# A gated graph layer on one core: five pieces of vector work change engines and tiles are aggregated two at a time

## The chip, the cores and the metric

The kernel runs on one core of a Trainium2 chip. The metric is the device time of one execution in microseconds (us), as the median of three runs. A core has a matrix engine (TensorE, PE in the profile, with PEld for its weight loads), a vector engine (VectorE, DVE), an engine for activations and copies (ScalarE, ACT), a general engine (GpSimd, POOL) and one that only issues transfers (SyncE, SP). Each engine works through its own queue in order, and the engines wait for each other through semaphores.

## What is computed

For each of 16 graphs there are 1024 nodes with 256 features (x), and one sparse 1024 x 1024 matrix A (adj) is shared by all. The weights W1 have two halves of 256 rows. For every edge from u to v with A[u, v] not zero, a gate is computed from both ends, and the node v sums the features of its neighbours once with A alone (m) and once with A times the gate (a):

```python
pre_u = jnp.einsum('bud,dk->buk', h_t, W1[:d])
pre_v = jnp.einsum('bvd,dk->bvk', h_t, W1[d:])
hidden = jax.nn.relu(pre_u[:, :, None, :] + pre_v[:, None, :, :] + b1)
S = jax.nn.sigmoid(jnp.einsum('buvk,ko->buvo', hidden, W2)[..., 0] + b2[0])
a_t = jnp.einsum('buv,bud->bvd', S * A_a, h_t)
m_t = jnp.einsum('uv,bud->bvd', A_m, h_t) * h_t
z_t = beta1 * h_t + beta2 * (jnp.einsum('bvd,de->bve', a_t, Wa) + ba) + beta3 * (jnp.einsum('bvd,de->bve', m_t, Wm) + bm)
```

The kernel visits only the edges that exist, about nine per node.

## The kernel before

**Blocks and tiles.** The 16 graphs are four groups (g) of four (GB), and the 1024 nodes are eight tiles of 128 (vt). A block k is one pair (g, vt), so there are 32 blocks. A block has two windows w of 64 nodes, and a window's edges fill five tiles of 128 edge slots (TW = 5). So a block has ten tiles, and the main loop (L684) runs over n = 0 to 319, one tile a step, with s = n % 10 as the place in the block. The order in which each engine gets its instructions is the order in which this loop writes them; `after(step, f)` puts a piece of work off to a later step, where `do(n)` writes it.

**A tile's way.** For tile n:

- `fetch` (L451): GpSimd issues an indirect transfer that gathers 128 rows of 8 KB from a table in DRAM into one of five SBUF buffers `fetched` (NF = 5). Half of a row is h W1[:D] of node u for four graphs, the other half is h of node u.
- `expand` (L518): two PE products of the 0/1 matrix `mark` with X give, for each slot, h W1[D:] + b1 of its node v, in a PSUM tile `pc` of two banks. There are two such tiles (psc, bufs=2).
- `gate` (L536): DVE adds the fetched half and `pc` into an SBUF tile `t` (L539), then takes, graph by graph, the positive part times the row W2 and its sum (L543, four instructions, each followed by one that reads the accumulator). ACT makes the sigmoid (L546) and four scaled copies (L549).
- `left_adj` (L527): ACT writes the other half of the weights `left`: the 0/1 columns `onehot` times the edge's value `val` (L533).
- `aggregate` (L551): PE multiplies `left` (32 columns per graph) with the fetched h, four or eight products a tile, into sums `acc` in PSUM. The profile counts each of these products twice, so a tile shows as x8 or x16.

In step n the loop writes: aggregate(n-1), then fetch(n+4) into the buffer that this has freed, then gate(n), left_adj(n+1), whatever was put off to this step, and expand(n+2). After these come the pieces of the block work:

- `halves(k+1)` (L409): X of the next block. PE computes h W1[D:] + b1 in two halves; ACT copies each to X, rounded for the PE (L418), and DVE takes the rest, that is the PSUM value minus X (L419, `low`). ACT copies both to their places in X (L422, L425). These are written at s = 0, 2, 3, 4, 6.
- `half_end`, `turn_over` (L565, L570): ACT copies finished sums from PSUM (L568), PE transposes them (L578), ACT copies the result to `LT` (L581), and DVE multiplies the m part with h transposed (L591, `times_h`).
- `block_end(k-1)` (L596), at s = 3 to 6: PE multiplies `LT` with Wm and Wa on top of a bias row (L608, `pz`); DVE forms z = beta1 h + pz in place in the SBUF tile `h_blk` (L612), and SyncE writes that to DRAM.
- `rows` (L391): for the tables of later groups, PE computes h W1[:D]; the last piece is written in step 231.
- `lists` (L236) finds the edges of a node tile, mainly on DVE. Four of the eight run before the main loop, the others within its first hundred steps. GpSimd also fetches the edge values (`fetch_val`, L338), two per step, as long as some are left.

So GpSimd had the transfers alone, and DVE had per block ten gates, two L419, two L591 and two L612.

Of the kernel before, what the change touches and what calls it, by code (L numbers as in the profile page):

```python
# [13 lines left out]
P = 128  # L14
# [3 lines left out]
def kernel(  # L18
# [390 lines left out]
    def halves(k):  # L409
        X = cuts[k] = big.tile([P, NW, GD], FR, name="X")  # L410
        low = one.tile([P, GD], FR, name="low")
        for h in range(2):
# [6 lines left out]
            after(step + 1, lambda c=c, p=p: nc.vector.tensor_tensor(  # L419
                low[:, c], p, X[:, 0, c].bitcast(FP), ALU.subtract))  # L420
        yield
        nc.scalar.copy(X[W:, 1, :], X[W:, 0, :].bitcast(FP))  # L422
        for w in range(NW):
            yield
            nc.scalar.copy(X[(1 - w) * W:(2 - w) * W, w, :], low[w * W:(w + 1) * W].bitcast(FP))  # L425
# [85 lines left out]

    marks, pcs, accs, evs, hbs, LTs, lefts = {}, {}, {}, {}, {}, {}, {}
# [14 lines left out]
    def left_adj(n):  # L527
# [4 lines left out]
        lefts[n] = wk.tile([P, 2, GB, 2, V], FP, name="left")  # L532
        nc.scalar.activation(lefts[n][:, :m, :, 0, :], onehot[:, i, o:o + m, :].unsqueeze(2).to_broadcast([P, m, GB, V]),  # L533
                             AF.Copy, scale=val[:, i, j:j + 1])

    def gate(n):  # L536
        k, g, vt, w, j = where(n)
        t = one.tile([P, GB, D], FP, name="t")
        nc.vector.tensor_tensor(t, fetched[n % NF][:, :GD].rearrange("p (b d) -> p b d", b=GB),  # L539
                                pcs.pop(n).rearrange("p (b d) -> p b d", b=GB), ALU.add)  # L540
# [6 lines left out]
        for b in range(GB):  # L547
            m = len(QUARTERS[j])
            nc.scalar.activation(lefts[n][:, :m, b, 1, :], lefts[n][:, :m, b, 0, :], AF.Copy, scale=gt[:, b:b + 1])  # L549

    def aggregate(n):  # L551
        k, g, vt, w, j = where(n)
        left, f = lefts.pop(n), fetched[n % NF]
        for i, q in enumerate(QUARTERS[j]):
# [4 lines left out]
            for b in range(GB):  # L559
                nc.tensor.matmul(accs[h][b * 2 * V:(b + 1) * 2 * V, r, :],  # L560
                                 left[:, i, b].rearrange("p k v -> p (k v)"), f[:, GD + b * D:GD + (b + 1) * D],
                                 start=first, stop=(j == q + 1), skip_group_check=True)
# [7 lines left out]
    def turn_over(k, w, q, step):  # L570
# [18 lines left out]
        def times_h():  # L589
            m = LT[:, :, :, 0, v]  # L590
            nc.vector.tensor_tensor(m, m, hTs[order[k]].rearrange("p b c n -> p c b n")[:, :, :, v], ALU.mult)  # L591
# [4 lines left out]
    def block_end(k):  # L596

        g, vt = order[k]
        hb = hbs[k]
        for h in range(2):  # L600
            for bb in range(2):
# [4 lines left out]
                for i, wt in enumerate((w_m, w_a)):  # L606
                    for c in range(DC):
                        nc.tensor.matmul(pz[:, bb * D:(bb + 1) * D], LTs[k][:, c, 2 * h + bb, i, :], wt[:, c, :],  # L608
                                         start=False, stop=(i == 1 and c == DC - 1), skip_group_check=True)

            def add(h=h, pz=pz):
                nc.vector.scalar_tensor_tensor(hb[:, 2 * h:2 * h + 2, :], hb[:, 2 * h:2 * h + 2, :], be1,  # L612
                                               pz.rearrange("p (b d) -> p b d", b=2), ALU.mult, ALU.add)
# [263 lines left out]
```

## Time and profile before

The median is 1183.41 us (1183.29 to 1184.95). The profiled execution has a span of 1195.2 us[...]. The main loop starts at 68.5 us (the first L539) and the last gate starts at 1174.2 us.

| group | times | mean, ns |
|---|---|---|
| L419 DVE, rest of h W1[D:] | 64 | 686 |
| L591 DVE, m times h (128x512) | 55 | 688 |
| L612 DVE, z | 62 | 744 |
| L533 ACT, left | 320 | 364 |
| L546 ACT, sigmoid | 320 | 298 |
| L549 ACT, four per tile | 1280 | 304 |
| L568, L581 ACT, copies from PSUM of 128x512 | 128 each | 587, 575 |
| L418 ACT, copy from PSUM to X, 128x512 | 64 | 583 |
| L453 POOL, issue of a gather | 320 | 1030 |
| L341 POOL, issue of an edge value fetch | 80 | 1046 |

In such a profile an engine's busy time is the union of its instructions' spans. Two instructions that follow each other overlap at their ends, so the distance from one start to the next says more about what an instruction costs its engine than its duration does. "Idle before" is the time that an engine stood still just ahead of a group, with the instruction whose end released it. A wait in the table costs time only if the waiting engine is the one that sets the pace at that place.

### The profile page before, as it was taken

Reading aid. Unit: us, or ns where it says so; the run is one execution under the profiler, and the core shown is the slowest. Engines: PE = TensorE matmul, PEld = TensorE weight load, DVE = VectorE, ACT = ScalarE, POOL = GpSimd, SP = SyncE. Lnnn points to the kernel's source line nnn. Section 1 sums busy time; section 2 is a strip of 40 time slices with the busy share of each in tenths; the row PEclk is TensorE's granted clock in tenths of the full one; section 3 lists DMA queues with packets and bytes.
Section 4 is the critical chain, followed back from the end, with each engine's and each line's share of the span. In section 5 each row is a group of like instructions: output and inputs, shape, how many; then the busy total and the mean of one; then the engine's idle time right before and its main releaser. Section 6 shows DMA issues by size and latency. Waiting matters only on the chain. (4 is left out here: it accounts for less than half of the span.)

```text
span 1195.2 us, 23788 instructions
## 1 busy us (share of the span) xinstructions
PE 1097.9 (92%) x7633; PEld 724.7 (61%) x7633; DVE 1066.9 (89%) x3515; ACT 840.4 (70%) x2498; POOL 426.1 (36%) x428
## 2 busy tenths in 40 slices
PE   7667988999889898999999999999999999999986
PEld 6544655666556565666666666666666666666653
DVE  8769879989988988899899999999999999999994
ACT  3346666677667665777777777787878777777873
POOL 1557652433263226333233333333333333333330
PEclk9968899999999999999999999999999999999998
DMA  9988889899979978999999999999999999999992
GB/s 279 312 307 261 258 319 333 315 336 377 320 254 373 361 244 302 357 384 360 351 329 379 359 331 371 362 356 386 358 367 345 356 324 326 326 341 328 335 340 76
DMA packets 147046, 391.39 MB, mean 327 GB/s; under 512 B 16752, under 2 KB 105328, under 8 KB 110704
## 3 DMA queue, kind: packets, MB, share of 16 engines
q0 software_dynamic: 50016, 300.50, 68.5%
q1 hardware_dynamic: 81616, 74.99, 19.6%
q10 hardware_dynamic: 15280, 14.29, 3.7%
q8 instruction: 63, 1.03, 0.3%
q14 instruction: 71, 0.58, 0.1%
HBM read 393.78 MB, written 50.33 MB: 372 GB/s over the span
## 5 line engine op out<-in xcount | busy, mean ns | idle before, releaser
L453 POOL DMA_INDIRECT fetched<-table,uidx x320 | 329.7, 1030 | 675.5 <-PE acc L560 509.6
L543 DVE SCALAR_TENSOR_TENSOR t<-t,w_b 128x256 f32<-128x256 f32 x1280 | 469.3, 422 | 20.1 <-ACT LT L581 0.5
L539 DVE TENSOR_TENSOR t<-fetched,pc 128x1024 f32<-128x1024 f32 x320 | 388.8, 1215 | 22.4 <-DMA fetched<-table,uidx 8.6
L560 PE MATMUL acc<-fetched,left 128*32 128x256 f32 x4096 | 334.2, 394 | 32.3 <-ACT left L549 16.8
L549 ACT ACTIVATE left<-left,gt 128x32 f32<-128x32 f32 (+1 forms) x1280 | 299.4, 304 | 10.4
L523 PE MATMUL pc<-X,mark 128*128 128x512 f32 x640 | 238.1, 454 | 21.1 <-DVE t L539 13.6
L560 PEld LDWEIGHTS acc<-fetched,left 128*32 128x32 f32 x4096 | 129.9, 110 | 177.2 <-issue 46.9
L546 ACT ACTIVATE gt<-sc,b_b 128x4 f32<-128x4 f32 x320 | 95.3, 298 | 140.5 <-DVE t L543 133.9
L523 PEld LDWEIGHTS pc<-X,mark 128*128 128x128 f32 x640 | 97.2, 191 | 156.6 <-issue 102.2
L608 PE MATMUL misc<-w_a,LT 128*128 128x256 f32 x496 | 127.3, 379 | 0.0
L608 PE MATMUL misc<-w_m,LT 128*128 128x256 f32 x496 | 127.1, 378 | 0.0
L384 PE MATMUL misc<-w_u,hT 128*128 128x256 f32 x448 | 109.2, 390 | 11.0 <-ACT few L298 3.6
L533 ACT ACTIVATE left<-onehot,val 128x128 f32<-128x128 bf16 (+1 forms) x320 | 116.5, 364 | 0.0
L384 PE MATMUL misc<-w_v,hT 128*128 128x256 f32 x448 | 107.9, 384 | 0.0
L543 DVE DVE_READ_ACCUMULATOR t<-t,w_b 128x1 f32 x1280 | 104.2, 81 | 0.0
L608 PEld LDWEIGHTS misc<-w_m,LT 128*128 128x128 f32 x496 | 93.7, 189 | 17.2
L384 PEld LDWEIGHTS misc<-w_u,hT 128*128 128x128 f32 x448 | 85.8, 195 | 27.3 <-issue 4.4
L608 PEld LDWEIGHTS misc<-w_a,LT 128*128 128x128 f32 x496 | 94.2, 190 | 12.8
L568 ACT COPY ev<-acc 128x512 f32<-128x512 f32 x128 | 75.1, 587 | 34.7 <-PE acc L560 26.8
L341 POOL DMA_INDIRECT val<-in_adjT_dram,vidx x80 | 83.6, 1046 | 33.4 <-issue 21.9
L384 PEld LDWEIGHTS misc<-w_v,hT 128*128 128x128 f32 x448 | 86.7, 194 | 14.3
L581 ACT COPY LT<-misc 128x512 f32<-128x512 f32 x128 | 71.1, 575 | 24.0 <-PE pc L523 12.0
(158 smaller groups left out, 830.9 us busy)
## 6 DMA issues: line engine op xcount, KB each, us to landing
h_blk<-in_x_dram SPq DMA_DIRECT2D x31, 512.0 KB
out_dram<-h_blk SPq DMA_DIRECT2D x31, 512.0 KB
hT<-in_xT_dram SPq DMA_DIRECT2D x28, 512.0 KB
table<-tab SPq DMA_DIRECT2D x26, 512.0 KB
table<-in_x_dram ACTq DMA_DIRECT2D x24, 512.0 KB
fetched<-table,uidx POOLq DMA_INDIRECT x320
table<-in_x_dram SPq DMA_DIRECT2D x8, 512.0 KB
table<-fetched SPq DMA_DIRECT2D x6, 512.0 KB
```

The costliest lines, as they stand in the source:

```text
L341: nc.gpsimd.indirect_dma_start(out=val[:, i, j:j + 1], out_offset=None, in_=adj_flat, in_offset=bass.IndirectOffsetOnAxis(ap=vidx[:, i, j: ...
L384: nc.tensor.matmul(p[:, bb * D:(bb + 1) * D], hT[:, 2 * h + bb, i, :], wt[:, i, :], start=(i == 0 and not begun), stop=(i == DC - 1), skip ...
L453: nc.gpsimd.indirect_dma_start(out=fetched[n % NF], out_offset=None, in_=table[g], in_offset=bass.IndirectOffsetOnAxis(ap=uidx[:, vt * NW ...
L523: nc.tensor.matmul(pcs[n][:, c], marks[n // TW][:, j * P:(j + 1) * P], cuts[k][:, w, c], start=True, stop=True)
L533: nc.scalar.activation(lefts[n][:, :m, :, 0, :], onehot[:, i, o:o + m, :].unsqueeze(2).to_broadcast([P, m, GB, V]), AF.Copy, scale=val[:, ...
L539: nc.vector.tensor_tensor(t, fetched[n % NF][:, :GD].rearrange("p (b d) -> p b d", b=GB), pcs.pop(n).rearrange("p (b d) -> p b d", b=GB), ...
L543: nc.vector.scalar_tensor_tensor(t[:, b, :], t[:, b, :], 0.0, w2_b, ALU.max, ALU.mult, accum_out=sc[:, b:b + 1])
L546: nc.scalar.activation(gt, sc, AF.Sigmoid, bias=b2_b)
L549: nc.scalar.activation(lefts[n][:, :m, b, 1, :], lefts[n][:, :m, b, 0, :], AF.Copy, scale=gt[:, b:b + 1])
L560: nc.tensor.matmul(accs[h][b * 2 * V:(b + 1) * 2 * V, r, :], left[:, i, b].rearrange("p k v -> p (k v)"), f[:, GD + b * D:GD + (b + 1) * D ...
L568: nc.scalar.copy(evs[q], accs.pop(q))
L608: nc.tensor.matmul(pz[:, bb * D:(bb + 1) * D], LTs[k][:, c, 2 * h + bb, i, :], wt[:, c, :], start=False, stop=(i == 1 and c == DC - 1), sk ...
```

## The change

Six edits are made together. (1) `left` times `val` goes from ACT to GpSimd, with four buffers in place of three. (2) The rest of h W1[D:]: ACT now copies the PSUM value to SBUF a second time (`low`), and GpSimd subtracts X from it; the first block keeps DVE. (3) `times_h` goes from DVE to GpSimd, but for the last block. (4) z: ACT copies pz to a new SBUF tile `z`, GpSimd scales h and adds; the products with Wa come ahead of those with Wm, so that the m part is needed later. (5) The sum of fetched half and `pc` is written over `pc` in PSUM, and the gate works there, in place. (6) Tiles are aggregated two at a time: in every even step n the loop writes aggregate(n-2) and aggregate(n-1), and the two fetches n+3 and n+4; in odd steps it writes neither. A piece of `halves` moves from s = 4 to s = 5.

The purpose is to take everything from DVE but the gates, to let GpSimd do elementwise work between its transfers, and to let PE change less often between kinds of products. GpSimd is given SBUF operands only, and the copies in (2) and (4) provide them.

```diff
@@ -408,7 +408,8 @@
 
     def halves(k):
         X = cuts[k] = big.tile([P, NW, GD], FR, name="X")
-        low = one.tile([P, GD], FR, name="low")
+        low = one.tile([P, GD], FP, name="low")
+        engine = nc.gpsimd if k else nc.vector
         for h in range(2):
             step = yield
             c = slice(2 * h * D, (2 * h + 2) * D)
@@ -416,13 +417,13 @@
             add_row(p, b1_p)
             half_product(p, hTs[order[k]], w_v, h, True)
             nc.scalar.copy(X[:, 0, c], p)
-            after(step + 1, lambda c=c, p=p: nc.vector.tensor_tensor(
-                low[:, c], p, X[:, 0, c].bitcast(FP), ALU.subtract))
+            nc.scalar.copy(low[:, c], p)
+            after(step + 1, lambda c=c: engine.tensor_tensor(low[:, c], low[:, c], X[:, 0, c].bitcast(FP), ALU.subtract))
         yield
         nc.scalar.copy(X[W:, 1, :], X[W:, 0, :].bitcast(FP))
         for w in range(NW):
             yield
-            nc.scalar.copy(X[(1 - w) * W:(2 - w) * W, w, :], low[w * W:(w + 1) * W].bitcast(FP))
+            nc.scalar.copy(X[(1 - w) * W:(2 - w) * W, w, :], low[w * W:(w + 1) * W])
 
     engines = mybir.EngineType
     main.enter_context(tc.manual_schedule(
@@ -529,15 +531,16 @@
         i = vt * NW + w
         m = len(QUARTERS[j])
         o = max(2 * j - 1, 0)
-        lefts[n] = wk.tile([P, 2, GB, 2, V], FP, name="left")
-        nc.scalar.activation(lefts[n][:, :m, :, 0, :], onehot[:, i, o:o + m, :].unsqueeze(2).to_broadcast([P, m, GB, V]),
-                             AF.Copy, scale=val[:, i, j:j + 1])
+        lefts[n] = wk.tile([P, 2, GB, 2, V], FP, name="left", bufs=4)
+        nc.gpsimd.tensor_scalar(lefts[n][:, :m, :, 0, :], onehot[:, i, o:o + m, :].unsqueeze(2).to_broadcast([P, m, GB, V]),
+                                val[:, i, j:j + 1], None, ALU.mult)
+
 
     def gate(n):
         k, g, vt, w, j = where(n)
-        t = one.tile([P, GB, D], FP, name="t")
-        nc.vector.tensor_tensor(t, fetched[n % NF][:, :GD].rearrange("p (b d) -> p b d", b=GB),
-                                pcs.pop(n).rearrange("p (b d) -> p b d", b=GB), ALU.add)
+        m = len(QUARTERS[j])
+        t = pcs.pop(n).rearrange("p (b d) -> p b d", b=GB)
+        nc.vector.tensor_tensor(t, fetched[n % NF][:, :GD].rearrange("p (b d) -> p b d", b=GB), t, ALU.add)
         sc = wk.tile([P, GB], FP, name="sc")
         for b in range(GB):
             nc.vector.scalar_tensor_tensor(t[:, b, :], t[:, b, :], 0.0, w2_b,
@@ -545,7 +548,6 @@
         gt = wk.tile([P, GB], FP, name="gt")
         nc.scalar.activation(gt, sc, AF.Sigmoid, bias=b2_b)
         for b in range(GB):
-            m = len(QUARTERS[j])
             nc.scalar.activation(lefts[n][:, :m, b, 1, :], lefts[n][:, :m, b, 0, :], AF.Copy, scale=gt[:, b:b + 1])
 
     def aggregate(n):
@@ -557,8 +559,8 @@
             if first:
                 accs[h] = psa.tile([P, 2, D], FP, name=f"acc{h}")
             for b in range(GB):
-                nc.tensor.matmul(accs[h][b * 2 * V:(b + 1) * 2 * V, r, :],
-                                 left[:, i, b].rearrange("p k v -> p (k v)"), f[:, GD + b * D:GD + (b + 1) * D],
+                nc.tensor.matmul(accs[h][b * 2 * V:(b + 1) * 2 * V, r, :], left[:, i, b].rearrange("p k v -> p (k v)"),
+                                 f[:, GD + b * D:GD + (b + 1) * D],
                                  start=first, stop=(j == q + 1), skip_group_check=True)
@@ -588,7 +590,7 @@
 
         def times_h():
             m = LT[:, :, :, 0, v]
-            nc.vector.tensor_tensor(m, m, hTs[order[k]].rearrange("p b c n -> p c b n")[:, :, :, v], ALU.mult)
+            (nc.vector if k == BS - 1 else nc.gpsimd).tensor_tensor(m, m, hTs[order[k]].rearrange("p b c n -> p c b n")[:, :, :, v], ALU.mult)
             if w == NW - 1 and q == 1:
                 del hTs[order[k]]
         after(step + 1, times_h)
@@ -597,23 +599,27 @@
 
         g, vt = order[k]
         hb = hbs[k]
+        z = big.tile([P, GB, D], FP, name="z", bufs=1)
         for h in range(2):
             for bb in range(2):
                 step = yield
                 if bb == 0:
                     pz = small("pz")
                     add_row(pz, bias_p)
-                for i, wt in enumerate((w_m, w_a)):
+                for i, wt in ((1, w_a), (0, w_m)):
                     for c in range(DC):
                         nc.tensor.matmul(pz[:, bb * D:(bb + 1) * D], LTs[k][:, c, 2 * h + bb, i, :], wt[:, c, :],
-                                         start=False, stop=(i == 1 and c == DC - 1), skip_group_check=True)
-
-            def add(h=h, pz=pz):
-                nc.vector.scalar_tensor_tensor(hb[:, 2 * h:2 * h + 2, :], hb[:, 2 * h:2 * h + 2, :], be1,
-                                               pz.rearrange("p (b d) -> p b d", b=2), ALU.mult, ALU.add)
+                                         start=False, stop=(i == 0 and c == DC - 1), skip_group_check=True)
+
+            sl = slice(2 * h, 2 * h + 2)
+            nc.scalar.copy(z[:, sl], pz.rearrange("p (b d) -> p b d", b=2))
+
+            def add(sl=sl):
+                nc.gpsimd.tensor_scalar(hb[:, sl], hb[:, sl], be1, None, ALU.mult)
+                nc.gpsimd.tensor_tensor(z[:, sl], hb[:, sl], z[:, sl], ALU.add)
             after(step + 1, add)
         after(step + 2, lambda: nc.sync.dma_start(
-            out[g * GB:(g + 1) * GB, vt * P:(vt + 1) * P, :].rearrange("b p d -> p b d"), hb))
+            out[g * GB:(g + 1) * GB, vt * P:(vt + 1) * P, :].rearrange("b p d -> p b d"), z))
         del hbs[k], LTs[k]
@@ -684,12 +690,15 @@
     for n in range(total + 2):
         k, s = divmod(n, T)
         if 1 <= n <= total:
-            aggregate(n - 1)
             fetch_val(2)
-            if n - 1 + NF < total:
-                fetch(n - 1 + NF)
-            if n % TW in (0, MID + 1):
-                half_end(n - 1, 0 if n % TW else 1)
+        if 2 <= n <= total and n % 2 == 0:
+            for i in (n - 2, n - 1):
+                aggregate(i)
+                if i + NF < total:
+                    fetch(i + NF)
+            for i in (n - 2, n - 1):
+                if i % TW in (MID, TW - 1):
+                    half_end(i, 0 if i % TW == MID else 1)
         if n < total:
             gate(n)
             if n + 1 < total:
@@ -741,7 +750,7 @@
             next(end)
             go(end, n)
             go(end, n)
-        if k + 1 < BS and s in (0, 2, 3, 4, 6):
+        if k + 1 < BS and s in (0, 2, 3, 5, 6):
             if s == 0:
                 parts = halves(k + 1)
                 next(parts)
```

## The prediction

> **What bounds the kernel now.** I read the page's busy line first, then its costliest groups, then the busy time by stage, then timelines of one block.
>
> The page, busy time and groups:
>
> ```profile
> PE 1097.9 (92%) x7633; PEld 724.7 (61%) x7633; DVE 1066.9 (89%) x3515; ACT 840.4 (70%) x2498; POOL 426.1 (36%) x428
> ...
> L453 POOL DMA_INDIRECT fetched<-table,uidx x320 | 329.7, 1030 | 675.5 <-PE acc L560 509.6
> L543 DVE SCALAR_TENSOR_TENSOR t<-t,w_b 128x256 f32<-128x256 f32 x1280 | 469.3, 422 | 20.1 <-ACT LT L581 0.5
> L539 DVE TENSOR_TENSOR t<-fetched,pc 128x1024 f32<-128x1024 f32 x320 | 388.8, 1215 | 22.4 <-DMA fetched<-table,uidx 8.6
> L560 PE MATMUL acc<-fetched,left 128*32 128x256 f32 x4096 | 334.2, 394 | 32.3 <-ACT left L549 16.8
> ```
>
> PE and DVE are both near full and hardly idle; POOL is idle two thirds of the time, waiting for PE to free a gather buffer. Which of the two sets the pace depends on the stage. Busy time by stretch (columns: length, then busy time and instructions of PE, PEld, DVE, ACT, POOL; granted clock; DMA share; GB/s):
>
> ```profile
> 68.50:532.70 464.20, 419.59 (x2841) 277.58 (x2841) 410.51 (x1365) 315.13 (x937) 198.70 (x195) 0.95 0.90 316
> 532.70:927.70 395.00, 386.92 (x2765) 253.67 (x2766) 363.46 (x1152) 306.13 (x922) 124.08 (x121) 1.00 0.98 358
> 927.70:1176.60 248.90, 237.07 (x1714) 149.58 (x1716) 239.62 (x765) 191.72 (x594) 78.53 (x77) 1.00 0.92 326
> ```
>
> The cuts are starts of blocks: 12 early blocks of 38.7 us (edge lists on DVE), 12 middle ones of 32.9 us (tables for later groups on PE) and 8 late ones of 31.1 us. Late, DVE is busy 96%; in the middle PE is busy 98%. The timelines of DVE and PE in a late block:
>
> ```profile
> 1083.31 1.22 DVE L539 TENSOR_TENSOR t<-fetched,pc 128x1024 f32<-128x1024 f32 x1
> 1084.56 0.42 DVE L543 SCALAR_TENSOR_TENSOR t<-t,w_b 128x256 f32<-128x256 f32 x1
> 1084.91 0.08 DVE L543 DVE_READ_ACCUMULATOR t<-t,w_b 128x1 f32 x1
> ...
> 1088.84 0.69 DVE L419 TENSOR_TENSOR low<-misc,X 128x512 fp32r<-128x512 f32 x1
> 1089.44 1.21 DVE L539 TENSOR_TENSOR t<-fetched,pc 128x1024 f32<-128x1024 f32 x1
> ...
> 1105.23 1.03 PE L608 MATMUL misc<-w_m,LT 128*128 128x256 f32 x4
> 1106.09 1.03 PE L608 MATMUL misc<-w_a,LT 128*128 128x256 f32 x4
> 1107.05 1.07 PE L560 MATMUL acc<-fetched,left 128*32 128x256 f32 x16
> 1108.05 0.73 PE L523 MATMUL pc<-X,mark 128*128 128x512 f32 x2
> 1108.62 1.03 PE L578 MATMUL misc<-ident,ev 128*128 128x128 f32 x8
> 1109.59 1.07 PE L560 MATMUL acc<-fetched,left 128*32 128x256 f32 x16
> ```
>
> From start to start, a gate costs DVE 1.25 for the sum and 4 x 0.35 = 1.40, so 2.65 us. L419 costs 0.60, and so (timeline) do L591 0.61 and L612 0.66. A block's DVE work is 26.5 + 2 x (0.60 + 0.61 + 0.66) = 30.2 of 31.1 us. On PE an aggregation costs 1.00 (x16) or 0.57 (x8), an expansion 0.57, two L608 groups 1.82, eight transposes 0.97. Per block: 6 x 1.00 + 4 x 0.57 + 10 x 0.57 + w_v 2 x 1.82 + four bias rows 0.92 + L608 4 x 1.82 + transposes 2.1 = 27.9 us; with two pieces of `rows`, 31.5. So DVE bounds the late blocks (30.2 of 31.1) and PE the middle ones (31.5 of 32.9), each with about 1 us of coupling.
>
> A third loop runs through the gathers. By the semaphores in the trace, a gather lands 6.3 us (late) to 6.9 us (middle) after its issue ends, on average; 5.5 us when the one before it had 1 to 2 us left to run. It lands only 2.5 to 1.9 us before its gate starts.
>
> [...]
>
> **The change part by part.**
>
> Off DVE: 2 x 1.87 = 3.7 us per block, for 31 blocks nearly. Left: 26.5 us.
>
> In place in PSUM: before shows DVE reading PSUM (L539 1215 ns, against 1219 ns for L244 of the same size from SBUF), so a read costs nothing; a write to PSUM is nowhere. Lower bound 0[...]. I take 0.1 us per tile, as reads show none of it: DVE 27.5 per block[...]. The edit also holds `pc` until the gate's end: expand(n+2), which waited for L539, now waits 1.4 us longer, and queued behind it on PE are that step's block pieces and expand(n+3). The gate of tile n+1 runs meanwhile on the other `pc`, and gate n+2 is due 2.65 us later, while an expansion takes 0.57. I cost it at nothing on DVE.
>
> ACT: off, 10 x 0.364 = 3.6 us; on, 4 copies of 128x512 at 0.58 (L418) = 2.3. 1.3 less of 24 (191.7/8); ACT stays below 26 us, also in the middle (306.1/12 = 25.5).
>
> POOL, per block: ten gathers 10.3 (L453); ten `left`; two subtractions, two m x h, two scalings and two sums of 512 columns. Bounds: DVE's 0.69 us for the same sum (L591) below[...]. I take 1.15 for the six two-input ones (6.9), 0.6 for the scalings (1.2), and 0.3 for a `left` of 64 or 128 elements (3.0; between the 0.16 us memset L205 and ACT's 0.36). Sum 21.4 us of 31 (18 to 25): not a bound. POOL's order matters more: in even steps two issues (2.1 us), then left(n+1), then the odd work. In the first 15 steps two value fetches per step (2.1 us) come on top: 1.0 + 2.1 + 1.1 = 4.2 us of the 4.4 us that those steps take.
>
> New waits. The Wm products of L608 wait for m x h on POOL, which ends 2.1 + 0.3 + 1.15 = 3.6 us after the pair's aggregation; PE reaches them after two expansions, a `halves` piece, a bias row and the Wa products, 0.57 + 2.05 + 0.57 + 0.23 + 0.87 = 4.3 us after it, so nothing; behind them is the next pair. ACT's L549 of tile n+1 waits for its `left`, 2.4 us after the aggregation, while that gate ends later than 4 us after it; behind L549 on ACT are copies and the next sigmoid: nothing. POOL's sums of z wait for ACT's copy of pz, and the next two issues stand behind them: up to 0.5 us at s = 6 and 8, in the range.
>
> PE: 16 records take 1.00 and 8 take 0.57, so a change of kind costs 0.14; five pairs save 0.7 per block. PE: 27.2 late, 30.8 middle.
>
> Pairing the gathers. Before: issue 1.0, landing 6.3, gate 2.65, sigmoid and scaling 1.3 (0.30 + the four L549 0.96), aggregation 1.0: 12.3 us over five tiles, 24.5 per block. After: the first gather of a pair is issued a step later, so the same chain must close over four tiles. With a nearly empty transfer queue (5.5): 11.5 us per four tiles, 28.8 per block; with 6.3 us, 30.6. This eats most of what DVE gives free.
>
> Sum. Late: bounds DVE 27.5, PE 27.2, gathers 28.8; plus the 1 us of coupling seen before: 29.9, gain 1.2 x 8 = 9.6. Middle: PE 30.8 plus 1.2: 32.0, gain 0.8 x 12 (less the last rows) = 9. Early: the six list blocks at 38 to 42 us hold 35 to 36 us of DVE work; 3.7 less brings it to 32, and PE's 32 to 33 with its throttled stretches takes over: gain 2.2 x 6 = 13. The other four: 0.5 x 4 = 2. The first two: POOL leaves nothing. Together 33.6: 1183.4 - 33.6 = 1150.
>
> **The rivals.**
>
> Gathers eat it: with late landings of 6.3 to 6.9 us the four-tile chain gives 30.6 to 32 per block, so late and middle stand still (gain 0 to 0.5), and only the early stage gains 15: 1168. For it: "DMA share" 0.98 in the middle, 358 GB/s. Against: at slices of the page up to 387 GB/s pass, and landing shortens as the queue empties.
>
> Slower: [...]a `left` at 0.6 us or more, and POOL's odd work delaying the two issues by 0.5 us per pair add 1.3 us per middle and 0.7 per late block, less a gain of 10 in the early stage: 15.6 + 5.6 - 10 = +11: 1195. For it: POOL issues wait behind sums that wait for ACT copies (L612's successor follows PE by a step); before, gathers had just 2 us in hand. Against: POOL is two thirds empty.
>
> More than I think: coupling falls too, since PSUM tiles of `misc` are now freed by ACT at once, not by DVE a step later ("DVE h_blk <- PE" waits of 20.6 us, "DVE low <- ACT" of 19.7 go); late 28.5, middle 31.3, early 20 less: 20.8 + 19 + 20: 1124.
>
> **How the numbers follow.** Chances: the forecast 0.5, gathers eat it 0.22, slower 0.2, more 0.08. The forecast's own spread (PSUM write cost, landing) is 20 us to both sides. 1120 to 1192 leaves out half of the slower case and the far end of the best one. Faster by over 0.2% (under 1181): 0.5 + 0.08 + 0.17 of the gather case = 0.75; same 0.06; slower 0.19.
>
> **What would show it.** L419, L591 and L612's successors on POOL at 1.1 to 1.2 us and `left` near 0.3; DVE's gate at 2.65 to 2.75 from start to start; late blocks of 29.9 and middle ones of 32.0 us; DVE busy below 92% late, with idle time ahead of L539's successor ended by the gather's transfer, above all in odd tiles; aggregation pairs closing in 1.9 us. Wrong would be: gates of 2.9 us or more, POOL busy over 80%, or PE waiting long ahead of expansions for DVE.

## The result, and the profile after

The changed kernel takes 1374.22 us (1372.83 to 1385.54), beside 1183.35 us for the kernel before in the same session: a ratio of 1.163 [1.158, 1.168], slower by 191 us. The forecast was 1150 us and its range ended at 1192.

The page of the changed kernel, busy time and groups (as before: busy us and mean ns of one | idle before, and what ended it):

```profile
PE 1102.5 (80%) x7633; PEld 761.5 (55%) x7633; DVE 1109.7 (80%) x3329; ACT 816.2 (59%) x2304; POOL 929.0 (67%) x996
...
L546 DVE SCALAR_TENSOR_TENSOR pc<-pc,w_b 128x256 f32<-128x256 f32 x1280 | 553.5, 432 | 65.8 <-ACT left L551 0.5
L543 DVE TENSOR_TENSOR pc<-fetched,pc 128x1024 f32<-128x1024 f32 x320 | 399.4, 1248 | 172.6 <-DMA fetched<-table,uidx 151.2
L454 POOL DMA_INDIRECT fetched<-table,uidx x320 | 330.6, 1033 | 304.1 <-PE acc L562 144.7
L525 PE MATMUL pc<-X,mark 128*128 128x512 f32 x640 | 249.2, 473 | 200.9 <-DVE pc L546 194.1
...
L535 POOL TENSOR_SCALAR left<-onehot,val 128x128 f32<-128x128 bf16 (+1 forms) x320 | 173.4, 550 | 14.2 <-issue 7.5
L546 DVE DVE_READ_ACCUMULATOR pc<-pc,w_b 128x1 f32 x1280 | 180.8, 141 | 0.0
```

DVE lost 186 instructions, and yet it is busy for 43 us more than before. No engine is near full over the span: DVE now waits 151 us for gathers (8.6 before), and PE 194 us for DVE ahead of its expansions.

The durations hardly say where DVE's time went (L546 432 ns against 422). The timeline of DVE in a late block does (start, length):

```profile
1256.33 1.26 DVE L543 TENSOR_TENSOR pc<-fetched,pc 128x1024 f32<-128x1024 f32 x1
1257.70 0.43 DVE L546 SCALAR_TENSOR_TENSOR pc<-pc,w_b 128x256 f32<-128x256 f32 x1
1258.05 0.14 DVE L546 DVE_READ_ACCUMULATOR pc<-pc,w_b 128x1 f32 x1
1258.23 0.43 DVE L546 SCALAR_TENSOR_TENSOR pc<-pc,w_b 128x256 f32<-128x256 f32 x1
...
1259.63 1.26 DVE L543 TENSOR_TENSOR pc<-fetched,pc 128x1024 f32<-128x1024 f32 x1
...
1264.22 1.23 DVE L543 TENSOR_TENSOR pc<-fetched,pc 128x1024 f32<-128x1024 f32 x1 [1.16 <-DMA fetched<-table,uidx]
```

The products start 0.53 us apart (1257.70 to 1258.23), where they were 0.35 apart. From sum to sum it is 3.30 us, with nothing in between. In before, two late sums with nothing but a gate between them lie 2.80 to 2.88 us apart.

The busy time by stage, with the same cuts by blocks (length; busy time of PE, PEld, DVE, ACT, POOL; granted clock; DMA share; GB/s):

```profile
70.20:622.70 552.50, 429.88 (x2824) 297.44 (x2823) 431.37 (x1295) 306.00 (x863) 383.11 (x404) 0.89 0.76 264
622.70:1083.20 460.50, 385.61 (x2763) 265.82 (x2764) 375.88 (x1082) 298.46 (x854) 316.00 (x337) 0.95 0.86 308
1083.20:1366.20 283.00, 232.82 (x1730) 153.94 (x1730) 248.90 (x719) 183.29 (x540) 203.98 (x219) 0.94 0.81 288
```

Early blocks take 46.0 us (38.7 before), middle ones 38.4 (32.9), late ones 35.1 (31.1, each without the last block). Over 12, 12 and 8 blocks that is 88 + 65 + 32 = 185 us: every stage has lost, the early one most. (The forecast had a gain in each: 15, 9 and 9.6.)

### The profile page after: what moved, and what is told of

Its sections match the earlier page's. It is cut to its first block, busy times and chain, and to the rows that moved or that the text cites. A ratio compares the mean times of both kernels' runs of the same rounds, so it can differ in the third digit from the quotient of the medians.

```text
span 1383.7 us, 24724 instructions
## 1 busy us (share of the span) xinstructions
PE 1102.5 (80%) x7633; PEld 761.5 (55%) x7633; DVE 1109.7 (80%) x3329; ACT 816.2 (59%) x2304; POOL 929.0 (67%) x996
## 4 chain that ended last, share of the span: by engine, by line
PE 29%; DVE 26%; DMA 21%; issue 11%; POOL 10%; ACT 2%; POOLq 0%; DVEq 0%; ACTq 0%
DMA fetched<-table,uidx 20%; DVE pc L546 13%; DVE pc L543 8%; PE misc L611 8%; PE acc L562 7%; PE misc L384 6%; PE pc L525 5%; POOL fetched L454 3%; POOL left L535 2%; POOL h_blk L618 2%; POOL val L341 2%; PE misc L580 1%; PE misc L388 1%; DVE cand L251 1%; DMA fetched<-in_adjT_dram 1%
## 5 line engine op out<-in xcount | busy, mean ns | idle before, releaser
L546 DVE SCALAR_TENSOR_TENSOR pc<-pc,w_b 128x256 f32<-128x256 f32 x1280 | 553.5, 432 | 65.8 <-ACT left L551 0.5
L543 DVE TENSOR_TENSOR pc<-fetched,pc 128x1024 f32<-128x1024 f32 x320 | 399.4, 1248 | 172.6 <-DMA fetched<-table,uidx 151.2
L525 PE MATMUL pc<-X,mark 128*128 128x512 f32 x640 | 249.2, 473 | 200.9 <-DVE pc L546 194.1
L562 PE MATMUL acc<-fetched,left 128*32 128x256 f32 x4096 | 302.0, 416 | 28.6 <-ACT left L551 28.1
L525 PEld LDWEIGHTS pc<-X,mark 128*128 128x128 f32 x640 | 106.5, 201 | 318.5 <-issue 202.8
L535 POOL TENSOR_SCALAR left<-onehot,val 128x128 f32<-128x128 bf16 (+1 forms) x320 | 173.4, 550 | 14.2 <-issue 7.5
L546 DVE DVE_READ_ACCUMULATOR pc<-pc,w_b 128x1 f32 x1280 | 180.8, 141 | 0.0
L384 PE MATMUL misc<-w_v,hT 128*128 128x256 f32 x448 | 119.0, 414 | 0.0
L421 POOL TENSOR_TENSOR low<-low,X 128x512 f32<-128x512 f32 x62 | 79.1, 1276 | 47.5 <-ACT low L420 47.5
L611 PEld LDWEIGHTS misc<-w_m,LT 128*128 128x128 f32 x496 | 94.7, 191 | 26.8 <-POOL LT L593 13.9
L384 PEld LDWEIGHTS misc<-w_v,hT 128*128 128x128 f32 x448 | 94.9, 212 | 17.8
## 6 DMA issues: line engine op xcount, KB each, us to landing
table<-in_x_dram SPq DMA_DIRECT2D x8, 512.0 KB, 11.9
```

The lines of the kernel that those rows point to most:

```text
L384: nc.tensor.matmul(p[:, bb * D:(bb + 1) * D], hT[:, 2 * h + bb, i, :], wt[:, i, :], start=(i == 0 and not begun), stop=(i == DC - 1), skip ...
L421: after(step + 1, lambda c=c: engine.tensor_tensor(low[:, c], low[:, c], X[:, 0, c].bitcast(FP), ALU.subtract))
L525: nc.tensor.matmul(pcs[n][:, c], marks[n // TW][:, j * P:(j + 1) * P], cuts[k][:, w, c], start=True, stop=True)
L535: nc.gpsimd.tensor_scalar(lefts[n][:, :m, :, 0, :], onehot[:, i, o:o + m, :].unsqueeze(2).to_broadcast([P, m, GB, V]), val[:, i, j:j + 1], ...
L546: nc.vector.scalar_tensor_tensor(t[:, b, :], t[:, b, :], 0.0, w2_b, ALU.max, ALU.mult, accum_out=sc[:, b:b + 1])
L562: nc.tensor.matmul(accs[h][b * 2 * V:(b + 1) * 2 * V, r, :], left[:, i, b].rearrange("p k v -> p (k v)"), f[:, GD + b * D:GD + (b + 1) * D ...
```

## The experiments

Twelve further kernels ran. The table collects them: the ratio to the kernel before on the same chip, and the length of a block by stage in one trace, from the starts of the tiles' sums (the last block left out). The four rows marked * ran on a chip on which the kernel before takes 1203.9 us, not 1183. It was not traced there, so up to 1.7% of what their blocks are longer may be the chip's. "One buffer for `tab`" below means the tile in which `rows` collects a table; its last use is in step 231, so the late blocks have none of it.

| kernel | ratio to before | early, middle, late |
|---|---|---|
| before | 1 | 38.7, 32.9, 31.1 |
| changed kernel (1 to 6) | 1.163 [1.158, 1.168] | 46.0, 38.4, 35.1 |
| without 5 | 1.164 [1.156, 1.172] | 45.9, 36.9, 36.4 |
| without 6 | 1.119 [1.112, 1.126] | 45.2, 34.7, 33.8 |
| 1 to 4 alone | 1.126 [1.118, 1.133] | 45.5, 34.6, 34.2 |
| 5 alone | 1.139 [1.130, 1.147] | 43.3, 36.7, 37.0 |
| 6 alone * | 1.035 and 1.052 | 41.0, 35.5, 32.6 (the run of 1.052) |
| sum in PSUM, products to SBUF * | 1.082 [1.074, 1.090] | 42.9, 35.2, 34.6 |
| sum in SBUF, products to PSUM * | 1.132 [1.122, 1.142] | 43.9, 37.2, 36.9 |
| 1 to 4, with products from PSUM to SBUF * | 1.090 [1.080, 1.101] | 44.7, 34.5, 32.8 |
| 1 alone | 1.044 [1.042, 1.046] | 41.8, 33.0, 31.5 |
| 2 to 4 alone | 1.096 [1.093, 1.098] | 42.7, 34.7, 34.6 |
| 3 alone, products with Wa first | 1.028 [1.026, 1.031] | 39.9, 33.1, 31.6 |
| changed, without one GpSimd reduction | 1.151 [1.148, 1.154] | 44.3, 37.8, 35.2 |

Each edit that ran on its own (1, 3, 5 and 6) makes the kernel slower, so do 2 to 4 together, and no version beats the one before. Edits 2 and 4 were not run apart. The costs do not add up (5 alone 13.9%, 1 to 4 alone 12.6%, all five together 11.9%, with pairs 16.3%): 5 takes away a cost that 1 to 4 bring, and brings another.

### The three parts apart

Edit 5 undone in the changed kernel (`tab` has one buffer here, for space):

```diff
-        t = pcs.pop(n).rearrange("p (b d) -> p b d", b=GB)
-        nc.vector.tensor_tensor(t, fetched[n % NF][:, :GD].rearrange("p (b d) -> p b d", b=GB), t, ALU.add)
+        t = one.tile([P, GB, D], FP, name="t")
+        nc.vector.tensor_tensor(t, fetched[n % NF][:, :GD].rearrange("p (b d) -> p b d", b=GB),
+                                pcs.pop(n).rearrange("p (b d) -> p b d", b=GB), ALU.add)
```

> The changed kernel with edit 5 alone undone: the sums and products of the gate lie in an SBUF tile t again (the tab tile has one buffer in place of two to make room). Theory P (the gate became slower on DVE because it reads and writes PSUM, 3.29 us from start to start where it was 2.81): the gate is back at 2.8 us or a little more, late blocks at 30 to 31 us, the whole at 1150 to 1190. Theory G (the gathers issued in pairs land too late): little is gained, 1320 to 1370, DVE keeps waiting for gathers. Theory S (GpSimd's share of SBUF): L546 reads two SBUF operands again and stretches beside GpSimd's work, above 0.5 us each, and the whole stays above 1250.

1374.98 us, ratio 1.164: nothing won. Of the three theories S fits best; the groups show why. The products, back in SBUF, take 561 ns on average in place of 432, and GpSimd's work has grown too:

```profile
L547 DVE SCALAR_TENSOR_TENSOR t<-t,w_b 128x256 f32<-128x256 f32 x1280 | 650.1, 561 | 33.1 <-ACT left L552 0.5
...
L535 POOL TENSOR_SCALAR left<-onehot,val 128x128 f32<-128x128 bf16 x192 | 134.5, 708 | 11.2 <-issue 7.2
L619 POOL TENSOR_SCALAR h_blk<-h_blk,be 128x512 f32<-128x512 f32 x62 | 111.0, 1791 | 0.0
```

In the changed kernel the same `left` takes 615 ns and the scaling 1553. So the in-place sum does keep DVE and GpSimd from stretching each other: with one input in PSUM the products stay at 432 ns beside GpSimd's work, with two in SBUF they go to 561. It only costs as much as it saves (ratios of 1.163 and 1.164).

Edit 6 undone in the changed kernel (the moved piece of `halves` stays moved, here and in the next run):

```diff
-        if 2 <= n <= total and n % 2 == 0:
-            for i in (n - 2, n - 1):
-                aggregate(i)
-                if i + NF < total:
-                    fetch(i + NF)
...
+            aggregate(n - 1)
+            fetch_val(2)
+            if n - 1 + NF < total:
+                fetch(n - 1 + NF)
```

> The changed kernel with edit 6 alone undone: one aggregation and one fetch in each step. Theory P: the gate stays at 3.29 us, so a block needs 32.9 us on DVE and at least 33.5 in all; 1280 to 1350, some 30 to 90 us less than the changed kernel, with DVE's waits for gathers gone. Theory G: nearly all of the loss comes back, 1180 to 1230.

1321.48 us, ratio 1.119: pairing costs 53 us. DVE's wait for gathers falls from 151.2 to 66.6 us, and the gate keeps its 3.29 us. Over tiles 120 to 309 of the changed kernel DVE stood still 14.0 us ahead of the sums of even tiles and 59.5 ahead of those of odd ones; without pairs it is 15.2 and 7.9. The odd tile is the one whose fetch is written a step later, as the prediction had it.

Both diffs together, so edits 1 to 4 alone (one buffer for `tab`):

> The changed kernel with edits 5 and 6 undone: only the moves to GpSimd and ACT remain (tab with one buffer). Theory P and theory G both: faster than before, DVE needs 28 us per block, 1120 to 1170. Theory S or a GpSimd that is too slow (78 us more busy time per hundred than forecast): 1200 to 1300, with L546 above 0.45 us or with gathers issued late.

1329.65 us, ratio 1.126, and so slower than any of the theories had it. DVE has 3.7 us per block less to do, but the products take 547 ns on average, and late blocks are 34.2 us. In these the products last 5.2 us per block longer than 422 ns each.

Edit 5 alone, in the kernel before (the first diff, reversed):

> The kernel before with edit 5 alone: sum and products over pc in PSUM, all else as before. Theory P: the gate at 3.29 us gives a block 32.9 + 3.7 = 36.6 us on DVE, the late blocks 37 us, the whole 1340 to 1400, about as slow as the changed kernel. Theory G or S: the gate alone costs little here, 1183 to 1230.

1345.09 us, ratio 1.139. The products start 0.525 us apart and the accumulator reads take 141 ns, as in the changed kernel, without any work on GpSimd. Late blocks are 37.0 us. A late gate here takes 3.18 us at the shortest, from its sum to whatever DVE does next, so DVE's work is at least 10 x 3.18 + 3.7 = 35.5. That leaves at most 1.4 us per block for the late release of `pc`, for which PE waits 190.7 us in all. The trace shows 0.7 us of it as a wait on DVE: ahead of L419 for ACT's copy to X, whose product stands behind the expansions in PE's queue. (In before, late blocks have no such wait.)

Edit 6 alone, in the kernel before (the second diff, reversed, and four buffers of `left`):

> The kernel before with edit 6 alone: tiles aggregated and gathers issued in pairs (left with four buffers). Theory G (the chain gather, gate, scaling, aggregation must close over four tiles in place of five): by the forecast's own sum 28.8 to 30.6 us per block, near DVE's 30.2, so DVE begins to wait for gathers: late blocks 32 to 34 us, the whole 1210 to 1270. If pairing costs only where the gate is slow: 1180 to 1200.

Two runs of 1246.5 and 1266.8 us beside 1203.9 for the kernel before on that chip: 3.5 to 5.2% slower, without an interval, and the trace is of the longer run, so its figures may be too high. In it DVE's wait for gathers is 50.1 us (8.6 before), and over tiles 120 to 309 the idle time is 43.3 us ahead of the sums of odd tiles and 8.9 ahead of those of even ones. The shorter run too is slower: pairing needs no change on DVE to do harm.

### Is it the read of PSUM or the write?

In the kernel before, the sum goes to PSUM and the products read it there, but write an SBUF tile that nobody reads:

```diff
-        t = one.tile([P, GB, D], FP, name="t")
...
+        t = pcs.pop(n).rearrange("p (b d) -> p b d", b=GB)
+        nc.vector.tensor_tensor(t, fetched[n % NF][:, :GD].rearrange("p (b d) -> p b d", b=GB), t, ALU.add)
+        junk = one.tile([P, D], FP, name="junk")
...
-            nc.vector.scalar_tensor_tensor(t[:, b, :], t[:, b, :], 0.0, w2_b,
+            nc.vector.scalar_tensor_tensor(junk, t[:, b, :], 0.0, w2_b,
```

> The kernel before with the sum over pc in PSUM, but the products, which nobody reads, in an SBUF tile of their own: L543 reads PSUM and writes SBUF. If it is the write to PSUM that spaces the products out (0.525 us from start to start in the PSUM kernels, 0.348 before): back at 0.35, the gate at 2.9, the whole 1190 to 1230, and what is left over before is the later release of pc. If it is the read: 0.52, 1330 to 1350.

1300.09 us, ratio 1.082, between what was expected for the write and for the read. The timeline:

```profile
1103.57 0.42 DVE L543 SCALAR_TENSOR_TENSOR junk<-pc,w_b 128x256 f32<-128x256 f32 x1
1103.92 0.08 DVE L543 DVE_READ_ACCUMULATOR junk<-pc,w_b 128x1 f32 x1
1104.04 0.42 DVE L543 SCALAR_TENSOR_TENSOR junk<-pc,w_b 128x256 f32<-128x256 f32 x1
```

Now the reverse: the sum stays in SBUF and the products are written over `pc`:

```diff
+        pc = pcs.pop(n).rearrange("p (b d) -> p b d", b=GB)
...
-            nc.vector.scalar_tensor_tensor(t[:, b, :], t[:, b, :], 0.0, w2_b,
+            nc.vector.scalar_tensor_tensor(pc[:, b, :], t[:, b, :], 0.0, w2_b,
```

> The kernel before with the sum in SBUF and the products written over pc in PSUM: L543 reads SBUF and writes PSUM, and pc is held as long as in the changed kernel. If it is the write: 0.52 us from start to start, 1330 to 1350. If it is the read: 0.35, and 1190 to 1230 for the later release of pc.

1360.5 us, ratio 1.132, the case of the write:

```profile
1152.89 0.43 DVE L544 SCALAR_TENSOR_TENSOR pc<-t,w_b 128x256 f32<-128x256 f32 x1
1153.24 0.14 DVE L544 DVE_READ_ACCUMULATOR pc<-t,w_b 128x1 f32 x1
1153.42 0.43 DVE L544 SCALAR_TENSOR_TENSOR pc<-t,w_b 128x256 f32<-128x256 f32 x1
```

From start to start a product takes 0.47 us when it reads PSUM, 0.53 when it writes it, 0.53 when it does both, and 0.35 in SBUF. The instruction itself is 0.42 to 0.43 long in all four. Three such distances lie within a gate. The fourth product behaves otherwise: in SBUF it is followed by L419, L591 or L612 after 0.35 us, but by the next sum only after 0.52; where the products read PSUM it is 0.35 for both, waits aside. So of the ten late gates of a block, with the products read from PSUM, the four that are followed by a sum grow by 0.20 us, the four followed by L591 or L612 by 0.37, and the two followed by L419 by 0.56 (with 0.15 of a wait for X). That is 3.4 us per block; measured are 34.6 - 31.1 = 3.5, of which the chip may have some. So in the late stage a microsecond more on DVE is about a microsecond more of the block: the prediction's reading of what bounds it holds.

### What the work on GpSimd costs

Edits 1 to 4 with the products read from PSUM and written to SBUF, so that no product has two SBUF inputs (the changed kernel without pairs, with the `junk` of above and one buffer for `tab`):

> All moves to GpSimd and ACT, no pairs, the sum over pc in PSUM and the products in SBUF: L547 has one SBUF input, so it should not meet GpSimd in SBUF, and writes no PSUM. If the write is the cost, the gate is at 2.9 us with no stretched L547, DVE needs 29 us per block, late blocks 30 to 31.5 us; the early blocks stay slow where left waits for GpSimd: 1170 to 1230. If the read is the cost: as without pairs, 1320.

1310.73 us, ratio 1.090, near the 1320 that stood for the read. No product is stretched: the median is 424 ns, and at the 90th percentile of each group that lies beside a GpSimd instruction it is 425 to 433. Against the same gate without edits 1 to 4 (1.082), late blocks fall from 34.6 to 32.8 us: DVE's relief does arrive there. But the early stage rises from 42.9 to 44.7, and the gain is gone. DVE waits 103 us for gathers, ACT 96 us for `left`, once 16.6 us. Block 10 takes 61 us, where it takes 39 without edits 1 to 4. The timeline of GpSimd around that place in the changed kernel:

```profile
536.37 0.63 POOL L535 TENSOR_SCALAR left<-onehot,val 128x128 f32<-128x128 bf16 x1
544.98 0.39 POOL L770 PARTITION_ALL_REDUCE longest<-rest  x1 [7.98 <-DVE pc L543]
552.47 0.61 POOL L535 TENSOR_SCALAR left<-onehot,val 128x128 f32<-128x128 bf16 x1 [7.10 <-issue]
553.07 1.26 POOL L421 TENSOR_TENSOR low<-low,X 128x512 f32<-128x512 f32 x1
```

and in the kernel before:

```profile
469.81 1.10 POOL L453 DMA_INDIRECT fetched<-table,uidx  x1 [1.18 <-PE misc L384]
471.12 0.33 POOL L761 PARTITION_ALL_REDUCE longest<-rest  x1 [0.20 <-issue]
472.24 1.03 POOL L453 DMA_INDIRECT fetched<-table,uidx  x1 [0.79 <-PE acc L560]
```

This one reduction over partitions, in step 100, is in both kernels. Between transfers it takes 0.33 us and no more. Between elementwise instructions GpSimd stands still for 8.0 us before it and 7.1 after it, and `left` and the gathers stand behind. To test it, the reduction is replaced, in the changed kernel, by two small transposes on PE and a maximum on DVE:

```diff
-            nc.gpsimd.partition_all_reduce(longest, rest, P, bass_isa.ReduceOp.max)
+            pt, mx = small("pl"), const.tile([P, 1], FP, name="mx")
+            nc.tensor.transpose(pt[:NT, :P], rest, ident)
+            nc.vector.tensor_reduce(mx[:NT], pt[:NT, :P], AX.X, ALU.max)
...
+            def turn():
...
+                nc.tensor.transpose(pu[:1, :NT], mx[:NT], ident[:NT, :NT])
+                nc.vector.tensor_copy(longest[:1], pu[:1, :NT])
+            after(n + 2, turn)
...
```

> The changed kernel, with the one PARTITION_ALL_REDUCE of GpSimd at step 100 replaced by two small PE transposes and a DVE maximum. Theory (it is the two standstills of GpSimd around this instruction, 7 to 8 us each, that make block 10 as long as 61 us): block 10 falls to about 43 us and the whole from 1374 to 1356 (ratio to before 1.148). Rival (the stall has another cause, an edge value or a transfer that comes late): 1370 to 1376, with block 10 still near 60.

1360.06 us, ratio 1.151 [1.148, 1.154] against 1.163 [1.158, 1.168]; block 10 falls from 61.0 to 46.1 us. So one instruction of 0.39 us costs some 14 us.

Then edits of the list one by one, in the kernel before. Edit 1 alone, its three lines in `left_adj` as in the diff of the change:

> The kernel before with edit 1 alone: left times val on GpSimd, four buffers. Theory (a GpSimd instruction with one tensor input disturbs the gates little; in the runs with all the GpSimd work a product beside a left alone took 0.42 us, 0.50 at worst): blocks of 31.1 us late grow by at most 0.5, and the one PARTITION_ALL_REDUCE at step 100 costs about 20 us, because GpSimd stood still 7.3 us before and 8.5 us after it in the runs with elementwise work on GpSimd: 1183 + 20 + 10 = 1213 (1200 to 1225). Rival (left on GpSimd is what holds the aggregations and the gathers back, the ACT waits for left of 114 us): over 1260, with late blocks of 33 us.

1235.84 us, above what the theory gave. Two of its terms hold: late blocks grow by 0.35 us, and block 10 by 20.4 (it has the two standstills, 6.8 and 9.2 us). What it missed lies in blocks 1, 2, 4 and 7, which grow by 2.0, 4.6, 5.7 and 7.8 us. (Blocks 6 and 9 fall by 2.6 and 2.7, the other early ones change by at most 1.) Edge value fetches are issued in all four, and where they are GpSimd's queue is full (blocks 0, 3, 6 and 9 have some too and do not grow, which stays open):

```profile
129.02 1.06 POOL L341 DMA_INDIRECT val<-in_adjT_dram,vidx  x1 [0.18 <-issue]
130.39 1.06 POOL L341 DMA_INDIRECT val<-in_adjT_dram,vidx  x1 [0.31 <-issue]
131.76 1.00 POOL L453 DMA_INDIRECT fetched<-table,uidx  x1 [0.30 <-PE acc L560]
132.79 1.06 POOL L533 TENSOR_SCALAR left<-onehot,val 128x128 f32<-128x128 bf16 x1
134.03 1.14 POOL L341 DMA_INDIRECT val<-in_adjT_dram,vidx  x1 [0.17 <-issue]
```

A step takes GpSimd 5.0 us here, without a real gap; in the kernel before it took 3.9 (a value fetch at 462.21, the same one of the next step at 466.13). A `left` of 128 columns takes 0.82 us on average, where the changed kernel, whose products have one SBUF input, has 0.62. What comes late is above all `left` itself. Two tiles of block 7 last 6.4 and 5.1 us (3.4 and 3.3 before), and the first of them shows the chain:

```profile
364.93 0.90 ACT L549 ACTIVATE left<-left,gt 128x16 f32<-128x16 f32 x4 [2.42 <-POOL left L533]
365.29 1.66 PE L560 MATMUL acc<-fetched,left 128*32 128x256 f32 x8 [2.16 <-ACT left L549]
371.22 0.69 DVE L419 TENSOR_TENSOR low<-misc,X 128x512 fp32r<-128x512 f32 x1 [2.97 <-ACT X L418]
```

ACT waits for `left`, PE's aggregation for ACT, and the product for X stands behind that in PE's queue, so that DVE waits for X. In the four blocks DVE's waits of more than 0.15 us come to 32.6 us (14.7 before), and only 2.8 of that is for gathers. The rival that was named ahead of this run, that `left` holds the aggregations back, is right here, though it expected this in late blocks too.

Edits 2 to 4 alone: the run of edits 1 to 4 with the kernel before's `left_adj`:

> The kernel before with edits 2, 3 and 4: the rest of h W1[D:], m times h and z on GpSimd; left stays on ACT, sums in SBUF, no pairs, one buffer for tab. Theory (a GpSimd sum of two SBUF tensors stops a DVE product of two SBUF tensors for nearly its whole 1.28 us: such products took 1.49 in place of 0.42): six such sums and two scalings per block stretch the gates by 6 us while 3.7 us of DVE work leave, so late blocks go from 31.1 to about 33.5 us; with 20 us for the one PARTITION_ALL_REDUCE: 1183 + 32 x 2.4 + 20 = 1280 (1260 to 1300). Rival (left on GpSimd is the cost, block work is nearly free there): under 1215.

1297.11 us, within what the theory gave: late blocks of 34.6 us, with 3.7 us less of DVE work. This is the largest part of the cost of edits 1 to 4. Two gates of a late block:

```profile
1079.56 1.22 DVE L543 TENSOR_TENSOR t<-fetched,pc 128x1024 f32<-128x1024 f32 x1
...
1082.45 1.22 DVE L543 TENSOR_TENSOR t<-fetched,pc 128x1024 f32<-128x1024 f32 x1
1083.78 1.04 DVE L547 SCALAR_TENSOR_TENSOR t<-t,w_b 128x256 f32<-128x256 f32 x1
...
1085.45 2.21 DVE L547 SCALAR_TENSOR_TENSOR t<-t,w_b 128x256 f32<-128x256 f32 x1
...
1087.76 1.22 DVE L543 TENSOR_TENSOR t<-fetched,pc 128x1024 f32<-128x1024 f32 x1
```

The first gate is undisturbed and takes 2.89 us, as do 32 of the 35 late gates of this run without a stretched product (three wait for something else); the second has two stretched products and takes 5.31. Ten undisturbed gates are 28.9 us, and the products of a late block last 5.6 us longer than 422 ns each: 34.5, the length of the block. For edits 1 to 4 alone it is 28.9 + 5.2 = 34.1 of 34.2.

And edit 3 alone, with the order of the products from edit 4: two sums per block on GpSimd (the reduction is kept here):

```diff
-            nc.vector.tensor_tensor(m, m, hTs[order[k]]
+            (nc.vector if k == BS - 1 else nc.gpsimd).tensor_tensor(m, m, hTs[order[k]]
...
-                for i, wt in enumerate((w_m, w_a)):
+                for i, wt in ((1, w_a), (0, w_m)):
```

> The kernel before with edit 3 alone, m times h on GpSimd, and the products with Wa ahead of those with Wm. Theory (each 1.28-us sum on GpSimd stops the gate's products for 0.5 to 1.1 us, depending on how much of it falls beside a product, while 0.61 us leave DVE): net -0.2 to +0.9 us per block, and 15 to 20 us for the PARTITION_ALL_REDUCE, which this kernel keeps: 1183 + 10 + 18 = 1211 (1195 to 1225). Rival (the prediction's way, GpSimd takes it for nothing): 1.2 us less in each late block, 1183 - 20 + 18 = 1181 or lower; late blocks of 29.9 us.

1215.66 us, as the theory had it. The timeline of a late block, with the lines of DVE and GpSimd:

```profile
1098.28 1.22 DVE L539 TENSOR_TENSOR t<-fetched,pc 128x1024 f32<-128x1024 f32 x1
...
1099.18 1.28 POOL L591 TENSOR_TENSOR LT<-LT,hT 128x512 f32<-128x512 f32 x1
...
1099.60 1.15 DVE L543 SCALAR_TENSOR_TENSOR t<-t,w_b 128x256 f32<-128x256 f32 x1
1100.68 0.08 DVE L543 DVE_READ_ACCUMULATOR t<-t,w_b 128x1 f32 x1
1100.68 0.41 DVE L543 SCALAR_TENSOR_TENSOR t<-t,w_b 128x256 f32<-128x256 f32 x1
```

GpSimd's sum began before the product, and the product is held until that sum is over (1100.46): 1.08 us to the next in place of 0.35, and the next starts 0.22 us after the sum's end. The DVE sum ahead of it, with one input in PSUM, ran beside GpSimd at its usual 1.22. Over the whole run, the products that lie beside `LT` and nothing else have a median of 1121 ns, all those beside nothing 421. The 0.61 us taken off DVE come back as 0.7, and late blocks go from 31.1 to 31.6 us. A `left` alone holds a product for little (median 422 ns, 502 at the 90th percentile, in the run of edit 1).

## Why the prediction was wrong

**What bounds the kernel: right for the late stage.** There it is DVE; the run with products read from PSUM shows its added time in the blocks about one for one. That PE bounds the middle stage no run tested by itself.

**"In place in PSUM" and "Left: 26.5 us": here the prediction failed most.** It took 0.1 us per tile for PSUM, and 27.5 us of gates per block. Measured are 3.29 us per gate, 32.9 per block: 0.64 us per tile over the 2.65 assumed. Two terms were too small.

- The gate itself: 0.24 us. The 2.65 counts 0.35 us for the last product, but the next sum starts 0.52 after it; and a sum that follows a gate is 1.33 us ahead of its first product, not 1.25. An undisturbed gate in SBUF among nothing but gates takes 2.89 us, 28.9 per block. In before this hid: six of ten gates are followed by other work, a late gate takes 2.67 us there and 2.81 else, and DVE's work is 31.0 of the 31.1 us. So the 3.7 us that leave DVE free no more than 2.1. Part of this was in sight: in the lines shown of before, two gates take from 1083.31 to 1088.84, 2.77 us each.
- PSUM: 0.41 us, four times the 0.1 us taken, which was the author's estimate: before had no DVE write to PSUM. "Reads show none of it" was drawn from the durations of L539 and L244. A duration does not hold this cost: it is 0.42 us for a product whose distance to the next is 0.35, 0.47 or 0.53. And L539 is one instruction of 1024 columns, with nothing of its kind behind it, while the gate has four short ones in a row, each with an accumulator read. The distances grew by 120 ns for a read (0.35 to 0.47 us) and 180 for a write (0.35 to 0.53).

**The late release of `pc`, "at nothing on DVE": nearly right in itself.** PE waits long ahead of expansions, the sign that was named for an error, but edit 5 alone leaves no more than 1.4 us per block for it and shows 0.7 on DVE, ahead of L419. In the changed kernel the pair's aggregation and its fetches stand behind that wait, so that there it is part of the next point.

**Pairing: the mechanism right, the size right only late, and by luck.** The sum put gathers at 28.8 us per block beside DVE's 27.5, so that they alone set the pace. As run, late blocks without pairs are gates of 32.9 and 0.9 of waits, 33.8. Pairs add 1.3 to it: DVE's waits for gathers go from 0.6 to 2.1 us per block. That is the difference of the two terms of the sum, but neither of them was as run. In the middle the sum had PE set the pace and gave pairs no cost; they add 3.7, 38.4 against 34.7. "Above all in odd tiles" was right. The rival "gathers eat it" named the cause, but as something that eats a gain, and there was no gain to eat. (The page's fastest slice moves 386 GB/s, not 387.)

**Contention: left out for edits 1 to 4.** The prediction did not ask what GpSimd's sums of edits 2 to 4 would do to gates in SBUF: 5.2 us per late block for edits 1 to 4 alone, with products of 547 ns in place of 422. That is why undoing 5 wins nothing: the gate has the choice between 0.53-us products in PSUM and products in SBUF that GpSimd's sums hold up.

**GpSimd "not a bound": right late, wrong early.** Per block, `left` takes 6 x 0.615 + 4 x 0.451 = 5.5 us (3.0 forecast), the two-input sums 6 x 1.28 = 7.7 (6.9) and the scalings 2 x 1.55 = 3.1 (1.2): with the gathers 26.6 us, not 21.4. The figure for a `left` had been drawn from a memset and from ACT; those for a sum and a scaling were the author's estimates, and in the trace of before GpSimd has neither. The prediction saw that the value fetches fill GpSimd in the first 15 steps ("POOL leaves nothing"), but then counted a gain of 13 us for the six list blocks, in which fetches go on. In place of it the early stage lost 88 us, the largest miss of any stage: DVE stands still 81 us there for gathers (1.6 before).

**Not seen at all: the reduction in step 100.** Some 14 us. In before nothing points to it, since it stands there between transfers, at 0.33 us.

**Still open.** The granted clock is 0.89, 0.95 and 0.94 by stage (0.95, 1.00, 1.00 before), and in late blocks of the changed kernel there are stretches of 3.4, once 6.8 and once 10.2 us, with a granted clock of 0.50, next to PE's idle time (the one from 1259.6 to 1263.1 us begins as a wait of 2.65 us of PE for DVE ends). Whether they add time or only accompany it was not separated. Of the early stage's 88 us, about 15 are the reduction; how the rest divides between slower gates, late gathers, late `left`, full queue and list work on DVE was not measured part by part. Nor was the piece of `halves` that moves to s = 5, which stays moved in the runs that undo edits of the changed kernel.

## What to carry to other kernels

Cost an engine's work by the distance from one start to the next, for the very chain of instructions and operand places that the change makes: a price read from a duration, or from one long instruction, says nothing of four short ones in a row (0.42 us long in each place, but 0.35, 0.47 or 0.53 apart). Before elementwise work goes to GpSimd, look at what DVE runs meanwhile: beside products with two SBUF inputs, a GpSimd sum took back as much as it relieved (0.7 us for 0.61), and moving those products to PSUM cost about as much as it spared (1.163 against 1.164). And price what is left on the first engine as it will stand: gates that follow each other took 2.89 us, where gates with other work behind them had taken 2.67. Last, an engine that is idle two thirds of the time may be the one whose promptness others live on: count what will stand ahead of each issue and each tile in its queue, in the fullest step and not on average.

## What the runs showed of the hardware

- A DVE product of 128x256 with an accumulator, and the read of it, follow each other at 0.35 us in SBUF, 0.47 with the input in PSUM and 0.53 with the output in PSUM, at the same duration of 0.42 to 0.43. The accumulator read takes 81 ns, and 141 when the output is in PSUM.
- A GpSimd sum of two SBUF tensors that has begun holds a DVE product of two SBUF inputs to its end: 1.08 us in place of 0.35 in the lines above, with a median duration of 1121 ns. It isn't a slowing of both in proportion: the GpSimd sum in those lines keeps its 1.28. But other GpSimd instructions grow in such runs too, a `left` from 0.62 to 0.82 (edit 1 alone), a scaling from 1.55 to 1.79 and a sum for z from 1.28 to 1.38 (the changed kernel without edit 5). A DVE sum with one input in PSUM stays at 1.22 (edit 3 alone).
- In seven runs in which GpSimd does elementwise work, the PARTITION_ALL_REDUCE has 6.8 to 8.6 us of standstill ahead of it, and the next elementwise instruction 7.1 to 9.8 (gathers between the two are issued at once, 0.20 us after the reduction in the run of edit 1). In three in which it only issues transfers by then (before, edit 5 alone, sum in PSUM with products to SBUF), the reduction waits 0.2 us. What GpSimd does in the standstills no run shows.
- On GpSimd a `tensor_scalar` with a scalar per partition takes 1.55 us for 512 float columns, more than a sum of two tensors of that size (1.28, both in the changed kernel).
